# A graph kernel with lists of edges: two more anchors in each list, other windows of nodes per slot, and U copied bank by bank

## The chip, the cores and the metric

The kernel runs on one core of one Trainium2 chip. The metric is the device time of one execution, in microseconds (us). Before the change it is 1675.7 us, the median of three runs (1673.89, 1675.7 and 1681.47).

## What is computed

`reference` takes x (8 graphs' worth of features on 2048 nodes, 64 features each) and one adjacency matrix, 2048 x 2048, which is symmetric, has every node's own edge, and holds about nine ones in a row. Four layers follow each other, each as `x = layernorm(x + layer(x))`:

```
layer 0: h = layernorm((x*w + b + x) @ W);  att = softmax over the neighbours of leaky(s1[i] + s2[j]);  elu(att @ h + h)
layer 1: per feature: softmax over the neighbours of softplus(x)*wa;  sum of it times softplus(x)
layer 2: relu(x @ W_self + mean over the neighbours of x @ W_neigh), layer norm
layer 3: four heads h = x @ Wh[k].T;  softmax over the neighbours of h_i . h_j;  leaky;  @ Wo.T;
         then the same attention once more with one head; leaky; layer norm
```

The layer that matters here is the third, above all its four heads: for each edge (i, j), graph and head the score h_i . h_j, its exponential, and the weighted sum of x_j.

## The kernel before, in words

**Tiles, groups, slots.** The 2048 nodes are cut into 16 tiles of 128 (`NT`, index `it`), a tile into two groups of 64 nodes (`NG`, `g`), a group into two blocks of 32 (`GB`). The edges of a group are listed in 5 slots (`GS`, `s`) of 128 places each. A slot may hold only edges of the nodes in its window, `WINDOWS[s]`, given as first and last-plus-one node of the group (line 69): 20, 22, 24, 22 and 20 nodes. Windows overlap, since how many places a node needs depends on the data. `blocks_of(s)` tells which blocks a window touches: the first two slots the first block, the last two the second, the middle slot (`MID`) both.

**The listing** (lines 364 to 430) runs once over the 16 tiles. It loads 128 rows of the adjacency matrix, makes `on` and the degree `deg` of each node on ScalarE (line 368), finds each node's neighbours with VectorE's MAX8 (380 to 387), and works out `offs`, the place at which each node's list begins. TensorE sums the degrees of the nodes ahead with a matmul of the constant matrix `before` (396); VectorE clips that and adds `base` (397, 398). The first block of a group is so packed from the first place on, without holes, and the second one up to the last place. From `offs` come the selection matrices `SelT` and `Sel` (405 to 417) and `src`, the node numbers of all places (419 to 427). `node_products` (line 287) makes layer 0's rows every second tile. The order of instructions in this stage is made by a scheduler from dependences and priorities. All later stages gather the rows of neighbours from tables in DRAM by `src` (`gather`, line 203, on GpSimd's queue), so they start when the listing is through.

**The stages behind it** are layer 0, layer 1, layer 2, the heads of layer 3, and its last attention (`fifth`). In all of them but the heads the work on a slot is done for whole blocks of 32 nodes, whatever its window.

**The heads** (line 1039 on) are written in an order by hand (`manual_schedule`), engine by engine. Steps are (it, g, s), with the slots of a group in the order `TURN = (0, 2, 1, 4, 3)`. Two steps make a pair, and five pairs (j = 0 to 4) an iteration, that is one tile. In window sizes before: pair 0 has slots of 20 and 24 nodes, pair 1 22 and 20, pair 2 22 and 20, pair 3 24 and 22, pair 4 20 and 22. A pair does this:

- `score` (line 1092), twice: TensorE multiplies the gathered rows (`xsT`, the stationary operand, 64 rows by 128 columns) with `U` of the window's nodes, four heads by `ni` nodes as moving columns (line 1101); ScalarE takes the exponential into `w` (1104), VectorE clips and masks it (1107).
- `turn` (1085): 16 transposes of the rows of the next pair (line 713) and their copy by ScalarE (1088).
- a quarter of the work on whole nodes (`QUARTERS`): `wo_all` in pair 0 (1193), `through_w` in pairs 1 and 2, `sides` in pairs 3 and 4 (their matmuls are all line 1064, of `quarters`).
- `back` (1112), twice: TensorE multiplies `w` of each block of the window (moving columns: four heads by the nodes of the window in that block) with the gathered rows (line 1126).

`sides` makes U for the next tile, two heads at a time: `pu` has two PSUM banks (first index j), each with both heads. ScalarE copies the first head out of both banks (1073), then VectorE the second head (1074). `pscore` has two buffers (`ps_s`), which the two scores of a pair and the quarters use in turn. `w` has four buffers of one pool.

`look` (line 1543) counts nodes that don't fit: those whose list begins ahead of its windows or ends behind them, and groups with more than 640 edges. If there is one, a slow path (line 1635 on) computes everything again.

Of the kernel before, what the change touches and what calls it, by code (L numbers as in the profile page):

```python
# [21 lines left out]
F32 = mybir.dt.float32  # L22
# [5 lines left out]
AF = mybir.ActivationFunctionType  # L28
ALU = mybir.AluOpType
# [3 lines left out]
P = 128  # L33
# [15 lines left out]
def kernel(ctx: ExitStack, tc: tile.TileContext, ins: dict, out: bass.AP):  # L49
    nc = tc.nc  # L50
# [16 lines left out]
    SL = 24  # L67

    WINDOWS = [(0, 20), (10, 32), (20, 44), (32, 54), (44, 64)]

    def blocks_of(s):

# [9 lines left out]
    MID = GS // 2  # L82
# [8 lines left out]
    ident = const.tile([P, P], F32, name="ident")  # L91
# [3 lines left out]
    ones_col = const.tile([P, 1], F32, name="ones_col")  # L95
# [35 lines left out]
    main = fast.enter_context(tc.tile_pool(name="main", bufs=1))  # L131
# [55 lines left out]
    room = main.tile([P, 2], F32, name="room")  # L187


    SelT = main.tile([P, NT, GE], FP8, name="SelT")  # L190
# [40 lines left out]
    aw = adj_.enter_context(tc.tile_pool(name="adjw", bufs=1, reuse_waits="tile"))  # L231
    ap_ = adj_.enter_context(tc.tile_pool(name="adjp", bufs=2, reuse_waits="tile"))
# [54 lines left out]
    def node_products(t0, wk, ps):  # L287
# [26 lines left out]
        for q, ph in enumerate(held):  # L314
# [21 lines left out]
    before = aw.tile([P, P], F32, name="before")  # L336
# [3 lines left out]
    block_no = aw.tile([P, P // GB, GB], F32, name="block_no")  # L340
# [5 lines left out]
    part = aw.tile([P, 4], F32, name="part")  # L346
# [17 lines left out]
    for it in range(NT):  # L364
# [70 lines left out]
    wk = l0.enter_context(tc.tile_pool(name="l0k", bufs=2, reuse_waits="tile"))  # L435
# [114 lines left out]
    with ExitStack() as l1:  # L550
        wp = l1.enter_context(tc.tile_pool(name="l1w", bufs=1, reuse_waits="tile"))
        wk = l1.enter_context(tc.tile_pool(name="l1k", bufs=2, reuse_waits="tile"))
# [116 lines left out]
        n = 0  # L669
# [127 lines left out]
    with ExitStack() as l2:  # L797
        wp = l2.enter_context(tc.tile_pool(name="l2w", bufs=1, reuse_waits="tile"))
        wk = l2.enter_context(tc.tile_pool(name="l2k", bufs=2, reuse_waits="tile"))
# [193 lines left out]
        with tc.manual_schedule(engines=engines):  # L993
# [49 lines left out]
    with early, ExitStack() as heads:  # L1043
        wk = heads.enter_context(tc.tile_pool(name="f3s", bufs=2, reuse_waits="tile"))
# [8 lines left out]
        Us, os, xss, xsTs, ws, pos, h2s, zs, dTs, Rs, hTs = ({} for _ in range(11))  # L1053
# [14 lines left out]
        def sides(it, h0):  # L1068
            pu = quarters(G, lambda h: xTs[it].rearrange("p (a n) -> p a n", n=P), (h0, h0 + 1))
            if h0 == 0:  # L1070
                Us[it] = wk.tile([P, NP, HN, P], F32, name="U")
            U = Us[it].rearrange("p (j a) h n -> p j a h n", j=2)
            nc.scalar.copy(U[:, :, :, h0], pu[:, :, 0])
            nc.vector.tensor_copy(U[:, :, :, h0 + 1], pu[:, :, 1])  # L1074

        TURN = (0, 2, 1, 4, 3)
        steps = [(it, g, s) for it in range(NT) for g in range(NG) for s in TURN]
# [14 lines left out]
        def score(k):  # L1092
            it, g, s = steps[k]
            i0, ni = g * GN + WINDOWS[s][0], WINDOWS[s][1] - WINDOWS[s][0]
            pscore = ps_s.tile([P, 2, CW], F32, name="pscore")
            xsT = xsTs.pop(k)
            for p in range(NP):
                for k_ in range(2):
                    half = slice(k_ * D, (k_ + 1) * D)
                    f0 = p * HN * ni  # L1100
                    nc.tensor.matmul(pscore[:, k_, f0:f0 + HN * ni].rearrange("p (h i) -> p h i", i=ni),  # L1101
                                     xsT[half, p], Us[it][half, p, :, i0:i0 + ni], start=True, stop=True)
            w = ws[k] = wk.tile([P, 2, NP, HN, ni], F32, name="w", bufs=4)
            nc.scalar.activation(w.rearrange("p k a h i -> p k (a h i)"), pscore[:, :, 0:NP * HN * ni], AF.Exp)  # L1104
            edge = Sel[:, it, g].rearrange("p q n -> p (q n)")[:, FROM[s]:FROM[s] + ni].unsqueeze(1).to_broadcast([P, NP * 2 * HN, ni])
            wt = w.rearrange("p k a h i -> p (k a h) i")
            nc.vector.scalar_tensor_tensor(wt, wt, 3.0e38, edge, op0=ALU.min, op1=ALU.mult)  # L1107
# [197 lines left out]
        with tc.manual_schedule(engines=engines):  # L1305
# [11 lines left out]
            for m in range(len(steps) // 2):  # L1317
                it, j = divmod(m, PER)
# [42 lines left out]
    with ExitStack() as fifth:  # L1361
# [17 lines left out]
        hss, hsTs, pes, ws, wxs, zs, stats, sums = ({} for _ in range(8))  # L1379
# [163 lines left out]
        def look():  # L1543
            many_recs(8, last_recs)
            nc.vector.tensor_reduce(nbad[:, 9:10], few[:, 0:NT - 1], AX.X, ALU.add)
            nc.vector.tensor_scalar(nbad[:, 9:10], nbad[:, 9:10], float((NT - 1) * RD), None, op0=ALU.not_equal)
            lack = fp.tile([P, 5, NT], F32, name="lack")
            nc.vector.tensor_tensor(lack[:, 0], listed, deg, ALU.not_equal)
            nc.vector.tensor_tensor(ends, offs, deg, ALU.add)
            nc.vector.tensor_scalar(lack[:, 1], ends, room[:, 1:2], None, op0=ALU.is_gt)  # L1550
            nc.vector.tensor_scalar(lack[:, 3], offs, room[:, 0:1], None, op0=ALU.is_lt)
            crowd = fp.tile([P, NG, GN], F32, name="crowd")
            nc.vector.tensor_copy(crowd, group.unsqueeze(2).to_broadcast(crowd.shape))
            pc = ps_t.tile([P, NT], F32, name="pt")
# [80 lines left out]
    with tc.If(bad > 0), ExitStack() as anyway:  # L1635
        main = anyway.enter_context(tc.tile_pool(name="gmain", bufs=1))
# [25 lines left out]
        with tc.tile_pool(name="adjp", bufs=3) as ap_, tc.tile_pool(name="adjps", bufs=4, space=PSUM) as aps:  # L1662
# [19 lines left out]
            deg = small.tile([P, NT], F32, name="deg")  # L1682
# [489 lines left out]
```

## Time and profile before

| | |
|---|---|
| median of three runs | 1675.7 us |
| the profiled execution | 1810.59 us, its span 1808.8 us |
| mean granted TensorE clock in it | 0.861 |
| busy: TensorE, VectorE, ScalarE, GpSimd | 1378.3, 1195.8, 905.6, 782.8 us |
| listing | from 0 to about 182 us |
| layers 0, 1, 2 | to about 455, 704 and 953 us |
| heads | from about 953 to 1425 us |
| last attention | to the end |

The profiled execution took 135 us more than the median run. Busy times are of each engine's instructions, waits not counted; "PE" is TensorE's matmuls, "PEld" its loads of the stationary operand, DVE VectorE, ACT ScalarE, POOL GpSimd, and L1101 is line 1101 of the kernel. A group of instructions is given as line, engine, operation, what it writes and reads, shape, count, and then busy time and mean duration, and behind the second bar the idle time of the engine ahead of them with what ended it. One fp32 matmul of the program is two MATMUL records in the trace.

### The profile page before, as it was taken

Reading aid. Unit: us, or ns where it says so; the run is one execution under the profiler, and the core shown is the slowest. Engines: PE = TensorE matmul, PEld = TensorE weight load, DVE = VectorE, ACT = ScalarE, POOL = GpSimd, SP = SyncE. Lnnn points to the kernel's source line nnn. Section 1 sums busy time; section 2 is a strip of 40 time slices with the busy share of each in tenths; the row PEclk is TensorE's granted clock in tenths of the full one; section 3 lists DMA queues with packets and bytes.
Section 4 is the critical chain, followed back from the end, with each engine's and each line's share of the span. In section 5 each row is a group of like instructions: output and inputs, shape, how many; then the busy total and the mean of one; then the engine's idle time right before and its main releaser. Section 6 shows DMA issues by size and latency. Waiting matters only on the chain.

```text
span 1808.8 us, 39940 instructions
## 1 busy us (share of the span) xinstructions
PE 1378.3 (76%) x16028; PEld 949.9 (53%) x16028; DVE 1195.8 (66%) x2973; ACT 905.6 (50%) x1863; POOL 782.8 (43%) x777
## 2 busy tenths in 40 slices
PE   4673455653489996888937999999999779889993
PEld 3662233331133332732216777777777657667773
DVE  5989378787576465754763666666667626656667
ACT  5763133535961233535653556555655424555564
POOL 0000666662464552656624333334334056656551
PEclk9665667666799998999967999999999969998897
DMA  6550665552126883256614656665656266666651
GB/s 185 184 160 24 182 179 175 174 175 60 70 105 214 305 309 126 94 153 177 184 46 119 160 155 164 161 160 156 170 155 165 76 198 171 186 179 176 182 152 44
DMA packets 157019, 280.71 MB, mean 155 GB/s; under 512 B 68732, under 2 KB 94332, under 8 KB 154748
## 3 DMA queue, kind: packets, MB, share of 16 engines
q0 software_dynamic: 56320, 189.44, 35.5%
q1 hardware_dynamic: 83866, 84.45, 15.8%
q10 hardware_dynamic: 16640, 4.20, 1.0%
q8 instruction: 128, 2.10, 0.5%
q14 instruction: 65, 0.53, 0.1%
HBM read 237.60 MB, written 40.42 MB: 154 GB/s over the span
## 4 chain that ended last, share of the span: by engine, by line
PE 48%; ACT 8%; DVE 7%; issue 5%; DMA 1%; another core or an unknown queue 1%; POOL 1%; SPq 0%; ACTq 0%; POOLq 0%; DVEq 0%
PE pscore L1101 9%; PE pa L605 6%; PE po L1126 5%; PE ps L1429 5%; PE po L1468 4%; PE pt L1406 3%; PE pa L660 2%; PE pt L713 2%; ACT w L1104 2%; PE pa L1003 2%; PE pscore L1064 2%; PE py L833 2%; PE pe L1399 2%; PE pscore L1193 2%; ACT xsT L1088 1%
## 5 line engine op out<-in xcount | busy, mean ns | idle before, releaser
L204 POOL DMA_INDIRECT xs<-xtab,src x160 | 172.9, 1081 | 282.0 <-PE po L1126 243.9
L204 POOL DMA_INDIRECT hs<-htab,src x160 | 153.1, 957 | 261.7 <-PE pe L455 182.9
L204 POOL DMA_INDIRECT hs<-ktab,src x160 | 158.6, 992 | 139.4 <-DMA utab<-hT 46.3
L605 PE MATMUL pa<-R,ET 128*128 128x512 bf16 x768 | 179.4, 390 | 49.9 <-POOL R L593 33.7
L1107 DVE SCALAR_TENSOR_TENSOR w<-w,Sel 128x640 f32<-128x640 f32 (+2 forms) x160 | 134.2, 875 | 104.7 <-ACT w L1104 104.5
L1104 ACT ACTIVATE w<-pscore 128x640 f32<-128x640 f32 (+2 forms) x160 | 113.6, 745 | 145.5 <-PE pscore L1101 139.9
L1101 PE MATMUL pscore<-U,xsT 64*128 64x80 f32 (+2 forms) x2560 | 163.6, 278 | 5.4 <-DVE U L1074 4.3
L605 PEld LDWEIGHTS <-ET 128*128 128x128 fp8e4 x768 | 74.7, 100 | 162.5 <-issue 83.3
L170 ACT ACTIVATE X<-X,ln_m,ln_r 128x64 f32<-128x64 f32 x256 | 87.2, 427 | 144.3 <-DVE ln_m L162 134.0
L1101 PEld LDWEIGHTS pscore<-U,xsT 64*128 64x128 f32 x2560 | 152.6, 191 | 11.6 <-DVE U L1074 6.9
L1126 PE MATMUL po<-w,xs 128*64 128x88 f32 (+2 forms) x3072 | 130.8, 237 | 14.4 <-DVE w L1107 5.3
L1126 PEld LDWEIGHTS po<-w,xs 128*64 128x64 f32 x3072 | 113.8, 139 | 48.0 <-DVE w L1107 25.6
L1468 PE MATMUL po<-hs,w 128*32 128x65 f32 x2048 | 87.3, 234 | 33.2 <-issue 25.3
L1429 PE MATMUL ps<-U,hsT 128*128 128x64 f32 x768 | 104.3, 287 | 9.0 <-ACT hsT L1407 4.8
L1429 PEld LDWEIGHTS ps<-U,hsT 128*128 128x128 f32 x768 | 102.8, 210 | 10.0 <-ACT hsT L1407 5.4
L204 POOL DMA_INDIRECT rs<-rtab,src x80 | 75.8, 948 | 63.4 <-PE pa L660 43.0
L614 DVE RECIPROCAL rec<-pa 128x256 f32<-128x256 f32 x32 | 54.4, 1734 | 64.6 <-PE pa L660 30.8
L1468 PEld LDWEIGHTS po<-hs,w 128*32 128x32 f32 x2048 | 70.8, 118 | 45.0 <-issue 33.4
L1407 ACT COPY hsT<-pt 128x512 f32<-128x512 f32 x96 | 52.5, 586 | 81.8 <-remote 46.4
L476 DVE TENSOR_TENSOR hs<-hs,w 128x1024 f32<-128x1024 f32 x80 | 91.8, 1213 | 1.2 <-ACT wm L464 0.4
L204 POOL DMA_INDIRECT rs<-ytab,src x80 | 76.9, 961 | 32.9 <-issue 17.1
L1516 ACT ACTIVATE z<-z,ln_m,ln_r 128x64 f32<-128x64 f32 x240 | 83.4, 432 | 14.7 <-DVE ln_m L1504 14.1
(634 smaller groups left out, 3087.4 us busy)
## 6 DMA issues: line engine op xcount, KB each, us to landing
at<-in_adj SPq DMA_DIRECT2D x16, 1024.0 KB
R<-itab SPq DMA_DIRECT2D x60, 256.0 KB
rtab<-r SPq DMA_DIRECT2D x16, 512.0 KB
ptab<-hp SPq DMA_DIRECT2D x16, 384.0 KB
hi<-ptab SPq DMA_DIRECT2D x16, 384.0 KB
ktab<-hb SPq DMA_DIRECT2D x16, 260.0 KB
X<-in_x ACTq DMA_DIRECT2D x16, 256.0 KB
htab<-H SPq DMA_DIRECT2D x16, 256.0 KB
```

The source lines that it names most:

```text
L170: nc.scalar.activation(v[:, b], v[:, b], AF.Identity, scale=rstd[:, k:k + 1], bias=nmr[:, k:k + 1])
L204: nc.gpsimd.indirect_dma_start(out=dst, out_offset=None, in_=table[:, :], in_offset=bass.IndirectOffsetOnAxis(ap=src[:, it, s, g:g + 1], a ...
L476: nc.vector.tensor_tensor(wx, wx, along(w[:, own].rearrange("p g b -> p (g b)")), ALU.mult)
L605: nc.tensor.matmul(po[h].rearrange("p a f -> p (a f)"), ET[:, jt, it * P:(it + 1) * P], R[:, jt, q, h].rearrange("p a f -> p (a f)"), star ...
L614: nc.vector.reciprocal(rec, po[h][:, 0])
L1101: nc.tensor.matmul(pscore[:, k_, f0:f0 + HN * ni].rearrange("p (h i) -> p h i", i=ni), xsT[half, p], Us[it][half, p, :, i0:i0 + ni], start ...
L1104: nc.scalar.activation(w.rearrange("p k a h i -> p k (a h i)"), pscore[:, :, 0:NP * HN * ni], AF.Exp)
L1107: nc.vector.scalar_tensor_tensor(wt, wt, 3.0e38, edge, op0=ALU.min, op1=ALU.mult)
L1126: nc.tensor.matmul(po[half, p, :, a - blk * GB:b - blk * GB], xs[:, f0:f0 + D], w[:, k_, p, :, a - WINDOWS[s][0]:b - WINDOWS[s][0]], start ...
L1429: nc.tensor.matmul(pscore[:, g, 2 * p:2 * p + 2], hsT[:, g, p], U[:, p, :, node_block(g, k)], start=False, stop=(p == NP - 1))
L1468: nc.tensor.matmul(po[node_block(g, k), j, b], w[:, g, t], hs[:, g, t], start=(s == BEGIN[k] and b == 0), stop=(s == END[k] and b == B // ...
L1516: nc.scalar.activation(v, v, AF.Identity, scale=r, bias=n)
```

## The change

Two things are changed.

**Windows and anchors.** The windows become 16, 18, 32, 18 and 16 nodes. So that every list falls into them, the first node at depth 16 or more in a block (depth counted from the group's outer edge) may not begin ahead of place 128, and that at depth 28 not ahead of place 256; in the second block the same holds from the other end. For this the listing has two more constant matrices (`far`), whose matmul with `deg` gives minus the degrees outside of the anchor, and `base` enters as a matmul of its own (`base_diag`) instead of an add. Per tile there are three fp32 matmuls of one column more on TensorE, one [128,1] ACTIVATE on ScalarE (`gap`), and on VectorE two scalar_tensor_tensor in place of one tensor_tensor. Ahead of the loop stand 20 instructions on VectorE (nine of them of 128x128) in place of one and one iota on GpSimd. `look` compares the end of the first block with the begin of the second one, with two small instructions more. In the heads, `w` of the middle slot gets a buffer of its own, and there is one.

**U bank by bank.** In `sides`, ScalarE copies one bank (both heads, p = 0 and 1 of U), VectorE the other one (p = 2 and 3).

```diff
-    WINDOWS = [(0, 20), (10, 32), (20, 44), (32, 54), (44, 64)]
+    ANCHORS = (16, 28)
+    WINDOWS = [(0, 16), (10, 28), (16, 48), (36, 54), (48, 64)]
...
-    base = aw.tile([P, 1], F32, name="base")
-    nc.vector.tensor_scalar(base, part[:, 3:4], float(GB), float(GE), op0=ALU.is_ge, op1=ALU.mult)
+    inward = aw.tile([P, NG, GN], F32, name="inward")
+    nc.gpsimd.iota(inward, pattern=[[0, NG], [1, GN]], base=0, channel_multiplier=0, allow_small_or_imprecise_dtypes=True)
+    inward = inward.rearrange("p g n -> p (g n)")
+    other = aw.tile([P, P], F32, name="other")
+    nc.vector.tensor_scalar(other, inward, -1.0, float(GN - 1), op0=ALU.mult, op1=ALU.add)
+    nc.vector.tensor_tensor(inward, inward, other, ALU.min)
...
+    for k, n in enumerate(ANCHORS):
+        far = aw.tile([P, P], F32, name=f"far{k}")
+        nc.vector.tensor_scalar(far, inward, float(n), None, op0=ALU.is_ge)
+        nc.vector.scalar_tensor_tensor(far, block_no.rearrange("p a b -> p (a b)"), part[:, 1:2], far, op0=ALU.is_equal, op1=ALU.mult)
+        nc.vector.tensor_scalar(depth[:, 4 + k:5 + k], depth[:, 0:1], float(n), -1.0, op0=ALU.is_lt, op1=ALU.mult)
+        nc.vector.tensor_scalar(far, far, depth[:, 4 + k:5 + k], None, op0=ALU.mult)
+        nc.vector.tensor_scalar(depth[:, 2 + k:3 + k], depth[:, 0:1], float(n), float(P * (k + 1)), op0=ALU.is_ge, op1=ALU.mult)
+        outer.append(far)
...
-        nc.tensor.matmul(poff, before, deg[:, it:it + 1], start=True, stop=True)
+        nc.tensor.matmul(poff, before, deg[:, it:it + 1], start=True, stop=False)
+        nc.tensor.matmul(poff, base_diag, ones_col, start=False, stop=True)
+        pouter = plist[:, CW // 2 - 2:CW // 2]
+        for k in range(2):
+            nc.tensor.matmul(pouter[:, k:k + 1], outer[k], deg[:, it:it + 1], start=True, stop=True)
+        gap = ap_.tile([P, 2], F32, name="gap")
+        nc.scalar.activation(gap[:, 0:1], pouter[:, 0:1], AF.Relu, bias=depth[:, 2:3])
         nc.vector.tensor_scalar(offs[:, it:it + 1], poff, -1.5 * GE, 2.0 * GE, op0=ALU.max, op1=ALU.min)
-        nc.vector.tensor_tensor(offs[:, it:it + 1], offs[:, it:it + 1], base, ALU.add)
+        nc.vector.scalar_tensor_tensor(gap[:, 1:2], pouter[:, 1:2], depth[:, 3:4], gap[:, 0:1], op0=ALU.add, op1=ALU.max)
+        nc.vector.scalar_tensor_tensor(offs[:, it:it + 1], gap[:, 1:2], depth[:, 1:2], offs[:, it:it + 1], op0=ALU.mult, op1=ALU.add)
...
-            U = Us[it].rearrange("p (j a) h n -> p j a h n", j=2)
-            nc.scalar.copy(U[:, :, :, h0], pu[:, :, 0])
-            nc.vector.tensor_copy(U[:, :, :, h0 + 1], pu[:, :, 1])
+            U = Us[it].rearrange("p (j a) h n -> p j a h n", j=2)[:, :, :, h0:h0 + 2]
+            nc.scalar.copy(U[:, 0], pu[:, 0].rearrange("p h a n -> p a h n"))
+            nc.vector.tensor_copy(U[:, 1], pu[:, 1].rearrange("p h a n -> p a h n"))
...
-            w = ws[k] = wk.tile([P, 2, NP, HN, ni], F32, name="w", bufs=4)
+            w = ws[k] = wk.tile([P, 2, NP, HN, ni], F32, name="w_mid" if s == MID else "w", bufs=1 if s == MID else 4)
...
-            nc.tensor.matmul(pc, crowd.rearrange("p g n -> p (g n)"), deg, start=True, stop=True)
-            nc.vector.tensor_scalar(lack[:, 4], pc, float(GE), None, op0=ALU.is_gt)
+            nc.vector.tensor_scalar(ends, ends, meet[:, 0:1], None, op0=ALU.mult)
+            nc.vector.scalar_tensor_tensor(ends, offs, meet[:, 1:2], ends, op0=ALU.mult, op1=ALU.add)
+            nc.tensor.matmul(pc, crowd.rearrange("p g n -> p (g n)"), ends, start=True, stop=True)
+            nc.vector.tensor_scalar(lack[:, 4], pc, 0.0, None, op0=ALU.is_gt)
```

More of the change, by code (lines that the diff above doesn't have):

```diff
@@ L187 @@
     room = main.tile([P, 2], F32, name="room")
+    meet = main.tile([P, 2], F32, name="meet")
     SelT = main.tile([P, NT, GE], FP8, name="SelT")
@@ L351 @@
                                    op0=ALU.is_equal, op1=ALU.mult)
-    base = aw.tile([P, 1], F32, name="base")
-    nc.vector.tensor_scalar(base, part[:, 3:4], float(GB), float(GE), op0=ALU.is_ge, op1=ALU.mult)
+    inward = aw.tile([P, NG, GN], F32, name="inward")
[4 more added lines that the diff above has]
+    nc.vector.tensor_tensor(inward, inward, other, ALU.min)
+    depth = aw.tile([P, 6], F32, name="depth")
+    nc.vector.tensor_scalar(depth[:, 1:2], part[:, 3:4], -1.0, float(GN - 1), op0=ALU.mult, op1=ALU.add)
+    nc.vector.tensor_tensor(depth[:, 0:1], depth[:, 1:2], part[:, 3:4], ALU.min)
+    nc.vector.tensor_scalar(depth[:, 1:2], part[:, 3:4], float(GB), -2.0, op0=ALU.is_ge, op1=ALU.mult)
+    nc.vector.tensor_scalar(depth[:, 1:2], depth[:, 1:2], 1.0, None, op0=ALU.add)
+    outer = []
+    for k, n in enumerate(ANCHORS):
[7 more added lines that the diff above has]
+    for k in range(2):
+        nc.vector.tensor_scalar(meet[:, k:k + 1], part[:, 3:4], float(GB - 1 + k), 1.0 - 2.0 * k, op0=ALU.is_equal, op1=ALU.mult)
+    base_diag = aw.tile([P, P], F32, name="base_diag")
+    nc.vector.tensor_scalar(depth[:, 5:6], part[:, 3:4], float(GB), float(GE), op0=ALU.is_ge, op1=ALU.mult)
+    nc.vector.tensor_scalar(base_diag, ident, depth[:, 5:6], None, op0=ALU.mult)
     over_one = aw.tile([P, 1], F32, name="over_one")
@@ L395 @@
         poff = plist[:, 0:1]
-        nc.tensor.matmul(poff, before, deg[:, it:it + 1], start=True, stop=True)
+        nc.tensor.matmul(poff, before, deg[:, it:it + 1], start=True, stop=False)
+        nc.tensor.matmul(poff, base_diag, ones_col, start=False, stop=True)
+        pouter = plist[:, CW // 2 - 2:CW // 2]
+        for k in range(2):
+            nc.tensor.matmul(pouter[:, k:k + 1], outer[k], deg[:, it:it + 1], start=True, stop=True)
+        gap = ap_.tile([P, 2], F32, name="gap")
+        nc.scalar.activation(gap[:, 0:1], pouter[:, 0:1], AF.Relu, bias=depth[:, 2:3])
         nc.vector.tensor_scalar(offs[:, it:it + 1], poff, -1.5 * GE, 2.0 * GE, op0=ALU.max, op1=ALU.min)
-        nc.vector.tensor_tensor(offs[:, it:it + 1], offs[:, it:it + 1], base, ALU.add)
+        nc.vector.scalar_tensor_tensor(gap[:, 1:2], pouter[:, 1:2], depth[:, 3:4], gap[:, 0:1], op0=ALU.add, op1=ALU.max)
+        nc.vector.scalar_tensor_tensor(offs[:, it:it + 1], gap[:, 1:2], depth[:, 1:2], offs[:, it:it + 1], op0=ALU.mult, op1=ALU.add)
         nc.vector.scalar_tensor_tensor(ends[:, it:it + 1], offs[:, it:it + 1], -2.0, deg[:, it:it + 1], op0=ALU.mult, op1=ALU.subtract)
```

## The prediction

> **What bounds the kernel now.** First the busy times by stretch: listing (two of its stretches), heads, last attention. Behind each engine's name in the heading stand its busy us and its instructions; then the granted clock.
>
> ```profile
> core 0: us, PE busy (x) PEld busy (x) DVE busy (x) ACT busy (x) POOL busy (x), PEclk, DMA share, GB/s
> 50.00:100.00 50.00, 35.86 (x255) 32.94 (x254) 40.59 (x195) 36.30 (x66) 0.00 (x0) 0.62 0.45 150
> 100.00:150.00 50.00, 28.67 (x175) 26.57 (x176) 47.26 (x227) 27.93 (x49) 0.00 (x0) 0.58 0.45 142
> 953.00:1425.00 472.00, 433.39 (x8538) 365.83 (x8538) 308.98 (x437) 270.85 (x372) 170.86 (x158) 0.98 0.58 153
> 1425.00:1808.70 383.70, 307.98 (x3924) 248.30 (x3924) 233.66 (x610) 184.94 (x457) 193.36 (x181) 0.87 0.55 155
> ```
>
> The listing is VectorE's: 47.3 of 50 us in its second third. The heads are TensorE's: 433 of 472 us at nearly full clock, while VectorE has 309 and ScalarE 271. So I ask for the heads' matmuls by shape.
>
> ```profile
> L1101 PE MATMUL pscore<-U,xsT 64*128 64x88 f32 x1024 | 70.2, 276 | 0.0
> L1101 PE MATMUL pscore<-U,xsT 64*128 64x80 f32 x1008 | 69.3, 278 | 4.3 <-DVE U L1074 4.3
> L1126 PE MATMUL po<-w,xs 128*64 128x88 f32 x1024 | 53.1, 246 | 1.7 <-DVE w L1107 1.7
> L1126 PE MATMUL po<-w,xs 128*64 128x48 f32 x1024 | 36.8, 225 | 2.2 <-DVE w L1107 1.8 <-issue 0.2
> L1101 PE MATMUL pscore<-U,xsT 64*128 64x96 f32 x496 | 33.5, 275 | 0.0
> ```
>
> The two lines that the windows touch behave differently. Per record, L1101 costs 69 ns busy at 80 and at 88 columns (and 68 at 96); L1126 costs 52 ns at 88 and 36 at 48. The start times of single matmuls say it more exactly. They run in twos side by side; from one such two to the next it is 111.8 ns in L1101 at 80, 88 and 96 columns alike, and in L1126 75.9 ns at 88, 69.2 at 80 and 58.3 at 48.
>
> Last the waits inside an iteration (waits of the heads, TensorE and VectorE), and how two of them look in time (timeline of pair 3 and of the end of pair 4):
>
> ```profile
> PE pscore L1064 <- ACT w L1104: 13.3, 32, 0.6
> PE pscore L1101 <- DVE U L1074: 4.3, 15, 0.4
> PE po L1126 <- DVE o L1110: 2.8, 5, 0.7
> DVE U L1074 <- ACT U L1073: 17.4, 30, 0.9
> ```
> ```profile
> 1243.44 1.46 ACT L1104 ACTIVATE w<-pscore 128x768 f32<-128x768 f32 x2 [0.72 <-PE pscore L1101]
> 1244.28 1.76 DVE L1107 SCALAR_TENSOR_TENSOR w<-w,Sel 128x768 f32<-128x768 f32 x2 [1.68 <-ACT w L1104]
> 1244.30 1.09 PE L1064 MATMUL pscore<-xT,G 64*64 64x256 f32 x16
> 1245.32 1.76 PE L1126 MATMUL po<-w,xs 128*64 128x48 f32 x48
> ...
> 1251.65 0.62 ACT L1073 COPY U<-pscore 128x512 f32<-128x512 f32 x1
> 1252.30 0.69 DVE L1074 COPY U<-pscore 128x512 f32<-128x512 f32 x1 [0.42 <-ACT U L1073]
> ...
> 1253.04 2.03 PE L1101 MATMUL pscore<-U,xsT 64*128 64x80 f32 x32 [0.28 <-DVE U L1074]
> ```
>
> In pair 3 the middle slot stands first: exponential, mask and `back` follow each other without slack (the mask of its first step ends at 1245.2, `back` starts at 1245.3). At the end of pair 4 VectorE's U copy waits for ScalarE's, and the next iteration's first score for VectorE's, once in 15 of 16 iterations.
>
> **What the Trainium skill says.** "TensorE: Matmul & The Clock Gate", section "Back-to-back issue gap", prices a warm matmul at N/2.4 + 2.5 ns. With N counted twice for fp32 this is 69.2 at 80 and 75.8 at 88 columns: the trace agrees. The same page, section "LDWEIGHTS (loading the stationary operand)": time goes by the columns of the weights, P/1.2, whatever the rows, so 107 ns for 128 and 53 for 64. The trace has 111.8 and 58.3, 5 ns more, as floors that don't move with the moving columns. So `score` is bound by loading its 128-column weights, and `back` has a floor of 58.3. "PSUM — Partial Sum Buffer", section "PSUM bank collisions raise a hardware error", says that two engines may not read one bank at once, other banks they may. The trace before shows the two U copies one behind the other; it can't show the second half.
>
> **The change, part by part.** Durations are of the profiled execution.
>
> *`back` (L1126).* Eight twos per block. Per group: two slots go from 80 to 64 columns (16 nodes x 4 heads), at 69.2 to the floor 58.3: 8 x 10.9 = 87 ns each. Two go from 88 to 72, 75.9 to 62.5 by the price: 8 x 13.4 = 107 ns each. The middle goes from 2 x 48 to 2 x 64 (55.8 by the price, under the floor): nothing. Sum 0.388 us a group, x32 = **-12.4 us** of TensorE's stream.
>
> *`score` (L1101).* 80 to 64 and 88 to 72 columns lie under the weights' 111.8; 96 to 128 gives 2 x 128/2.4 + 2.5 = 109.2, also under it: **0**. Bounds: if time went by columns, 32 fewer per group x 8 x 0.83 ns x 32 = -6.8; if the 128 columns ran beside nothing, +1 us.
>
> *Exponential and mask.* Their rows (640: 702 and 821 ns; 704: 755 and 889; 768: 811 and 957) give 0.85 and 1.06 ns a column; so 512: 0.60 and 0.69, 576: 0.65 and 0.75, 1024: 1.02 and 1.23 us. They lie beside TensorE except where it waits. By pair, medians of 13 to 16 iterations, us from the pair's first score:
> - Pair 0 (16, 32): the long mask comes second and ends at about 4.68 (was 4.47); its `back` is due at 4.86. Only -0.09, from `back`.
> - Pair 1: TensorE doesn't wait; -0.19.
> - Pair 2: the quarter waits for the first exponential (-0.10). Its second `back` waits for VectorE's copy of `po` behind both masks (ends 5.58, `back` at 5.75); exponential and masks shorter move it -0.35. With its own -0.09: -0.44.
> - Pair 3 (32, 18): the long one is first. Exponential +0.21, mask +0.27, and `back` stands right behind: +0.48; -0.11 from the second `back`: **+0.37**.
> - Pair 4: quarter -0.10, `back` -0.19, and the U wait.
>
> *U.* By the order of the changed program VectorE's copy still waits for ScalarE's, so the copies stay in a row. But the next score's first four matmuls now need ScalarE's bank alone, the other four VectorE's. Pair 4 would last 5.67 without the wait and lasts 6.05: 0.38. Afterwards ScalarE's copy ends at 5.07, VectorE's at about 5.86; the score starts at 5.36 and comes to its fifth matmul at 5.36 + 0.06 + 4 x 0.112 = 5.87. The wait goes, -0.38; by the waits' table 0.29 to 0.46. If VectorE came 0.3 later, a third of it would remain. Pair 4: -0.67.
>
> Sum per iteration: -0.09 - 0.19 - 0.44 + 0.37 - 0.67 = -1.02, x16 = **-16.3 us**. Of it -12.4 is stream, +7.7 the long slot ahead, and -11.6 shorter waits. `w_mid`'s one buffer costs nothing: its last reader is five steps back. If it did wait, TensorE would.
>
> *Listing.* VectorE: nine 128x128 instructions at about 0.2 us and ten small ones at 0.07, then 16 x 0.07: 2.5 + 1.1 = 3.6 us on the engine that bounds the stage (the iota on GpSimd is 0.27 us, and ready at 5 us). TensorE: three one-column products per tile, each two records with two 128-column loads, 0.22 us at full and 0.45 at half clock, +0.7 to 1.3 us between degree and `offs`. A new wait: `gap` on ScalarE waits for TensorE, and in its queue the next tile's `on` (2.0 us) and the ET copies stand behind it; VectorE then waits for `gap` with the MAX8s behind it. While MAX8s can fill, this is hidden; in the last two tiles nothing is left to fill (VectorE waits 3.8 us for `offs` in three places already): 2 x 1.5 = 3. The scheduler also puts the stage in another order. I take **+6.6 us**, with ends at 0 (the new order happens to be better) and +16 (1 us a tile).
>
> *`look`.* Two small instructions, 0.15 us each: +0.3 at most. *Gathers:* as many rows of the same size. 0.
>
> *Do the lists fit?* By the kernel's formulas on the reference's adjacency, no node falls outside its windows, before or after.
>
> **Sum:** -16.3 + 6.6 + 0.3 = -9.4: 1810.6 becomes 1801 in the profiled execution. That one is 135 us above the median, and nothing shows where. TensorE's stream keeps exact multiples of its clock in the profile, so I carry the difference over unscaled: 1675.7 - 9.4 = **1666**.
>
> **Rivals.**
> *Listing outweighs (slower).* VectorE standing at `gap` behind a 2.0 us `on`. It decides from (16.3 + 8.4)/16 = 1.5 us a tile; at 2.0 it is +32 - 16 = 1692. For it: the clock there is 0.6, and VectorE has only 3 us of slack in 50. Against: ScalarE is busy 28 of 50, and 2 us is the worst case.
> *The waits don't shrink (same).* The delay of the middle slot comes also in pair 0 and the waits in pairs 2 and 4 are set by semaphores, not by durations: -12.4 + 7.7 - 3 + 7 = 1675.
> *`score` shrinks too (faster):* -6.8 more, 1659. Against: three widths, one spacing.
> *The change doesn't do what it says:* a list overflows, and the slow path runs: thousands of us.
>
> **How the numbers follow.** Forecast 0.50 (1661 to 1672 by itself), `score` shrinks 0.12, waits don't shrink 0.24, listing outweighs 0.13, slow path 0.01. Half a per cent, 8.4 us, is about what a measurement can tell: 1667.3 to 1684.1 is "same". Faster: 0.34 + 0.12 = 0.46; same: 0.16 + 0.21 + 0.02 = 0.39; slower: 0.11 + 0.03 + 0.01 = 0.15. Both signs of the main doubt, and the listing's ends, give 1653 to 1681.
>
> **What would show it.** Right: L1126 at 64 columns with 58 ns and at 72 with 62; L1101 with 112 at every width; pair 3 longer, pairs 2 and 4 shorter; no wait of L1101's first score on U; heads about 16 us shorter, listing about 7 longer. Wrong: a spacing above 112 at 128 columns; pair 0 with a wait on the mask; a listing of over 200 us.

## The result: slower by 0.6%

The changed kernel takes **1688.46 us** (median of 12 runs, 1682.16 to 1693.28), the kernel before 1676.84 us (12 runs, 1673.89 to 1684.15): ratio 1.0060 [1.0042, 1.0077], or +10 us [+7, +13]. The prediction was 1666 us, in a range from 1653 to 1681.

One thing no number below can be read without: the kernel before takes 1674 to 1684 us on the chips of this comparison and of runs e8b to e17 ("the faster chips"), and 1811 to 1839 us on the one chip of runs e0 to e7 ("the slower chip") and in the profile that the prediction was worked out on. The table therefore sets the profile of the changed kernel beside a second profile of the kernel before, run e8b, which stands at the same level.

| us | before (e8b) | after | difference |
|---|---|---|---|
| start to the first gather of layer 0 (the listing) | 186.4 | 202.5 | +16.1 |
| from there to the heads' first score | 741.9 | 743.3 | +1.4 |
| heads, to the last product of `back` | 424.6 | 414.3 | -10.3 |
| to the end | 322.5 | 325.4 | +2.9 |
| span | 1675.3 | 1685.5 | +10.2 |

The second row and the last but one are not effects of the change: in eleven profiles on the faster chips, with either set of windows, these stretches are 742 to 746 and 321 to 325 us. Each column is one execution, and others differ by some us. In seven profiles of the changed listing the first gather starts at 197.5 to 202.8 us, in five of the old one at 184.5 to 189.2. The heads of the change take 413 to 420 us in five profiles on the faster chips, those of before 423 to 425 in four. An iteration of the heads (one tile) has a median of 26.53 us in e8b and 25.90 after, which is 10 us in sixteen.

The busy times by stretch, of the changed kernel (columns as before: behind each engine's name its busy us and instructions, then the granted clock):

```profile
core 0: us, PE busy (x) PEld busy (x) DVE busy (x) ACT busy (x) POOL busy (x), PEclk, DMA share, GB/s
50.00:100.00 50.00, 36.96 (x252) 33.37 (x252) 40.51 (x193) 35.03 (x65) 0.00 (x0) 0.57 0.48 154
100.00:150.00 50.00, 35.41 (x196) 33.44 (x193) 38.14 (x185) 26.49 (x49) 0.00 (x0) 0.57 0.41 131
...
945.50:1360.50 415.00, 405.06 (x8530) 347.37 (x8530) 301.74 (x436) 272.23 (x372) 166.60 (x157) 0.99 0.65 174
1360.50:1685.50 325.00, 280.51 (x3924) 233.71 (x3924) 234.79 (x613) 183.22 (x457) 192.92 (x181) 0.90 0.64 183
```

and the heads of the kernel before at the same level (e8b):

```profile
928.00:1353.00 425.00, 415.70 (x8530) 357.19 (x8530) 309.63 (x436) 276.34 (x372) 173.23 (x157) 0.99 0.64 170
```

In the heads TensorE is busy 416 of 425 us before and 405 of 415 after: its busy time fell by 10.6 us, the stage by 10. In the listing VectorE is busy for *less* of the stretch from 100 to 150 us than in either profile of before (38.1 of 50 us where it was 47.3), though it has more to do: it stands and waits.

The heads' matmuls by shape in the changed kernel:

```profile
L1133 PE MATMUL pscore<-U,xsT 64*128 64x64 f32 x1024 | 70.7, 277 | 1.3 <-ACT xsT L1120 1.1 <-issue 0.2
L1133 PE MATMUL pscore<-U,xsT 64*128 64x72 f32 x1024 | 68.6, 272 | 0.0
...
L1158 PE MATMUL po<-w,xs 128*64 128x72 f32 x1024 | 44.7, 229 | 0.5 <-DVE w L1139 0.5
L1158 PE MATMUL po<-w,xs 128*64 128x64 f32 x1024 | 43.5, 227 | 5.4 <-DVE o L1142 4.7 <-DVE w L1139 0.7
L1158 PE MATMUL po<-w_mid,xs 128*64 128x64 f32 x1024 | 36.9, 225 | 3.1 <-DVE w_mid L1139 2.8
L1133 PE MATMUL pscore<-U,xsT 64*128 64x128 f32 x512 | 36.6, 284 | 0.0
```

L1133 costs about 70 us per 1024 records at 64, 72 and 128 columns alike, as L1101 did at 80, 88 and 96: from one two to the next it is 112 ns everywhere. L1158 went from 53.1 to 44.7 us at the slots 1 and 3; its spacing is 62 to 63 ns at 72 columns and 58 at 64.

Where VectorE waits in the listing (first 200 us; us in total, times, longest), before (e8b):

```profile
DVE SelT L406 <- ACT apart L405: 5.4, 4, 2.4
DVE offs L397 <- PE pl L396: 3.6, 4, 3.0
```

and after:

```profile
DVE offs L428 <- ACT gap L427: 12.2, 10, 2.6
DVE SelT L438 <- ACT apart L437: 10.5, 7, 3.0
```

VectorE waited for the offsets in four places, 3.6 us (3.0 of it in one); now it waits in ten, 12.2 us, and 5.1 us more for `apart`, which comes out of the offsets. That is 13.7 us more in these two rows, a part of it given back in others: up to the first gather VectorE's busy time rose by 6.1 us (149.8 to 155.9) and its idle time by 10.

### The profile page after: what moved, and what is told of

The parts are those of the page before. It is cut to its first block, busy times and chain, and to the rows that moved or that the text cites. A ratio compares the mean times of both kernels' runs of the same rounds, so it can differ in the third digit from the quotient of the medians.

```text
span 1685.5 us, 40154 instructions
## 1 busy us (share of the span) xinstructions
PE 1322.5 (78%) x16124; PEld 928.4 (55%) x16124; DVE 1195.7 (71%) x3010; ACT 910.0 (54%) x1879; POOL 780.4 (46%) x778
## 4 chain that ended last, share of the span: by engine, by line
PE 45%; DVE 11%; ACT 5%; issue 3%; POOL 3%; DMA 1%; SPq 0%; POOLq 0%; ACTq 0%; DVEq 0%
PE pscore L1133 9%; PE pa L637 6%; PE po L1158 6%; PE pscore L1096 4%; PE pt L745 3%; PE pa L692 3%; PE ps L1461 3%; PE py L865 2%; PE po L1500 2%; PE pscore L1225 2%; PE pt L1438 2%; PE pa L1035 1%; ACT z L902 1%; POOL hs L206 1%; DVE pr L1447 1%
## 5 line engine op out<-in xcount | busy, mean ns | idle before, releaser
L1133 PE MATMUL pscore<-U,xsT 64*128 64x64 f32 (+2 forms) x2560 | 162.3, 276 | 1.3 <-ACT xsT L1120 1.1
L1133 PEld LDWEIGHTS pscore<-U,xsT 64*128 64x128 f32 x2560 | 151.5, 190 | 5.4 <-ACT xsT L1120 1.3
L1136 ACT ACTIVATE w<-pscore 128x512 f32<-128x512 f32 (+1 forms) x128 | 79.7, 624 | 86.4 <-PE pscore L1133 84.9
L1139 DVE SCALAR_TENSOR_TENSOR w<-w,Sel 128x512 f32<-128x512 f32 (+1 forms) x128 | 92.3, 722 | 35.2 <-ACT w L1136 32.1
L1461 PE MATMUL ps<-U,hsT 128*128 128x64 f32 x768 | 96.6, 273 | 1.5 <-ACT hsT L1439 1.5
L1461 PEld LDWEIGHTS ps<-U,hsT 128*128 128x128 f32 x768 | 95.3, 197 | 1.8 <-ACT hsT L1439 1.7
L1035 PE MATMUL pa<-Y,ET 128*128 128x512 bf16 x384 | 90.2, 384 | 0.0
L1158 PE MATMUL po<-w,xs 128*64 128x64 f32 (+1 forms) x2048 | 83.1, 228 | 5.9 <-DVE o L1142 4.7
L1158 PEld LDWEIGHTS po<-w,xs 128*64 128x64 f32 x2048 | 70.4, 138 | 31.4 <-issue 16.8
L1120 ACT COPY xsT<-pt 128x1024 f32<-128x1024 f32 x80 | 80.9, 1012 | 9.8 <-PE pt L745 9.7
L1500 PE MATMUL po<-hs,w 128*32 128x65 f32 x2048 | 73.7, 226 | 4.6 <-DVE w L1473 4.6
```

Of the source, the lines that this page charges most:

```text
L1120: nc.scalar.copy(unflipped(xsT), pt.rearrange("p k s a n -> p k (s a) n"))
L1158: nc.tensor.matmul(po[half, p, :, a - blk * GB:b - blk * GB], xs[:, f0:f0 + D], w[:, k_, p, :, a - WINDOWS[s][0]:b - WINDOWS[s][0]], start ...
L1461: nc.tensor.matmul(pscore[:, g, 2 * p:2 * p + 2], hsT[:, g, p], U[:, p, :, node_block(g, k)], start=False, stop=(p == NP - 1))
L1500: nc.tensor.matmul(po[node_block(g, k), j, b], w[:, g, t], hs[:, g, t], start=(s == BEGIN[k] and b == 0), stop=(s == END[k] and b == B // ...
```

## Two theories

**A, the listing outweighs.** The three added products and `gap` lie in a chain that every tile goes through, and take more than the heads give. **B, the heads fail.** The listing costs the 6.6 us that were predicted, and the narrower windows and the U copies give nothing. Every ratio is to the kernel before, run beside it on the same chip; beside e0 to e3 the kernel before took 1831 us, beside e4 to e7 1818.

## The experiments

**e0, the kernel before again.**

> The kernel before once more, for a profile that stands near its median. Both theories: about 1677 us. Theory A (the listing outweighs): the first gather of layer 0 at about 185 us as in the first profile, so 17 us ahead of the changed kernel's 202.5, and an iteration of the heads of about 26 us, so that the heads win some 6 us of the 17 back. Theory B (the heads give nothing): the first gather at about 195 us, and an iteration of the heads no longer than the changed kernel's 25.5 us.

1838.2 us and not 1677, first gather at 189.2 us, heads 476.8 us. So the first profile was no accident of one execution: on this chip all 21 runs of the kernel before took 1822 to 1839 us. The waits that the prediction priced are here again (waits of TensorE in the heads):

```profile
PE pscore L1064 <- ACT w L1104: 15.5, 41, 0.6
...
PE po L1126 <- DVE w L1107: 5.0, 6, 1.3
...
PE pscore L1101 <- DVE U L1074: 4.0, 14, 0.4
```

**e1 and e17, the listing alone**: the changed kernel with the windows and copies of before.

```diff
-    WINDOWS = [(0, 16), (10, 28), (16, 48), (36, 54), (48, 64)]
+    WINDOWS = [(0, 20), (10, 32), (20, 44), (32, 54), (44, 64)]
...
```

> The kernel before with the anchors in the listing and the new comparison in the last check, but with the windows and the U copies of before. Theory A: the first gather at about 202 us and +17 us, ratio 1.010. Theory B: +6.6 us, ratio 1.004, as predicted for the listing.

> The listing of the change with the windows and U copies of before, once more. On a chip where the kernel before takes 1677 us, from the traces: +16 us in the listing and nothing elsewhere, ratio 1.0095. On the slower kind 1.0087 as before.

e1: 1.0087 [1.0061, 1.0114], +16 us. e17: 1.0116 [1.0092, 1.0140], +19.5 us [+15, +23], first gather at 202.1 us, heads 423.7 us as before. On the slower chip and on the faster ones the listing alone costs two to three times what was predicted; on the faster ones that is more than the whole change loses (1.0060), on the slower one the intervals overlap. Theory A holds; B's listing is refuted. Between e17 and the whole change lie some 9 us that the rest of the change wins, so the heads don't give nothing either.

**e2 and e15, the U copies alone**, in the kernel before.

```diff
-            U = Us[it].rearrange("p (j a) h n -> p j a h n", j=2)
-            nc.scalar.copy(U[:, :, :, h0], pu[:, :, 0])
-            nc.vector.tensor_copy(U[:, :, :, h0 + 1], pu[:, :, 1])
+            U = Us[it].rearrange("p (j a) h n -> p j a h n", j=2)[:, :, :, h0:h0 + 2]
+            nc.scalar.copy(U[:, 0], pu[:, 0].rearrange("p h a n -> p a h n"))
+            nc.vector.tensor_copy(U[:, 1], pu[:, 1].rearrange("p h a n -> p a h n"))
```

> The kernel before with only the U copies changed to one bank for each engine. The prediction's mechanism (the next score's fifth matmul waits instead of its first): -0.38 us in 15 of 16 iterations, -6 us, ratio 0.9965. If VectorE's copy still comes too late: 0, ratio 1.000.

> The kernel before with the U copies bank by bank, once more. On a chip where the kernel before takes 1677 us its trace has no wait of the first score for U: ratio 1.000. If the copies give something apart from that wait (or the chip is of the slower kind and the wait is there): 0.997.

e2: 0.9993 [0.9977, 1.0010]. In its trace pair 4 is 0.36 us shorter (6.13 to 5.77), as predicted, and pair 0 behind it 0.14 longer (6.26 to 6.40): the first exponential of pair 0 starts 1.84 us behind the first score, where it was 1.49. The interval leaves out the predicted 0.9965. e15: 0.9983 [0.9974, 0.9992], -2.9 us; pair 4 goes from 5.00 to 4.78, pair 0 stays. The wait for U, which the expectation of e15 missed on the faster chips, was there, on the loads of the stationary operand (waits of PEld in the heads of e8b), and it is gone in e15 and in the changed kernel:

```profile
PEld pscore L1101 <- DVE U L1074: 4.8, 15, 0.3
```

So the mechanism is right on both levels, and its size on the faster chips is 0.22 us an iteration and not 0.38.

**e3, the change without the U copies, and e4, the changed kernel again.**

> The changed kernel with the U copies of before. Theory A: 6 us longer than the changed kernel, 1694 us, ratio 1.010, if the U copies win what was predicted. Theory B: 1688 us or less, ratio 1.006, with the bank-by-bank copies worth nothing.

> The changed kernel itself beside the kernel before on this chip, for a profile that can be laid beside those of the parts. If the parts of the change add up (listing 1.0087, windows 0.999, U copies 0.9993): ratio 1.007. If the first comparison is the right one everywhere: 1.006. An iteration of the heads no more than 0.4 us shorter than the kernel before has it.

e3: 1.0078 [1.0053, 1.0104]. e4: 1.0071 [1.0046, 1.0096], the first comparison again. The intervals are too wide to tell the copies' part from these two.

**e5, `gap` on VectorE**, which takes ScalarE's queue out of the chain.

```diff
-        nc.scalar.activation(gap[:, 0:1], pouter[:, 0:1], AF.Relu, bias=depth[:, 2:3])
+        nc.vector.tensor_scalar(gap[:, 0:1], pouter[:, 0:1], depth[:, 2:3], 0.0, op0=ALU.add, op1=ALU.max)
```

> The changed kernel with the first step of the gap on VectorE (an add and a maximum in one instruction) in place of ScalarE. Theory A (VectorE waits behind ScalarE's queue in every tile): some 8 to 13 us of the listing's 16 come back, ratio to the kernel before 0.999 to 1.002, first gather at about 190 us. Theory B (the added instructions of VectorE and the other order of the stage are what costs): no gain or 1 us lost, ratio 1.006 to 1.008.

1.0112 [1.0078, 1.0147], first gather at 206.0 us (197.5 in e4). Nothing comes back: VectorE now waits for the products themselves (waits of VectorE in the listing):

```profile
DVE SelT L438 <- ACT apart L437: 15.1, 7, 5.3
DVE gap L427 <- PE pl L425: 11.8, 9, 1.8
```

This speaks against theory A in its first form, the queue behind ScalarE's `on`. e5 alone doesn't settle it, since the scheduler gave VectorE another order of instructions in it; e12 below does, with `gap` left on ScalarE. The second form of theory A is: the products are late.

**e6, another order of slots, and e7, without a long slot.**

```diff
-        TURN = (0, 2, 1, 4, 3)
-        OPEN, CLOSE = (0, 2), (1, 3)
+        TURN = (0, 4, 2, 1, 3)
+        OPEN, CLOSE = (0, 4), (1, 3)
```

> The changed kernel with the slots of a group in the order 0, 4, 2, 1, 3, so that the middle slot is first in pair 1 and second in pair 3 (it was second in pair 0 and first in pair 3). If the long slot ahead costs what pair 3 shows (0.5 us an iteration) and pair 1 has the slack that it shows, where TensorE waits for no mask: -8 us against the changed kernel, ratio to before 1.002. If the loss follows the slot into pair 1: no change, 1.007.

```diff
-    WINDOWS = [(0, 16), (10, 28), (16, 48), (36, 54), (48, 64)]
+    WINDOWS = [(0, 20), (10, 28), (20, 44), (36, 54), (44, 64)]
```

> The changed kernel with windows of 20, 18, 24, 18 and 20 nodes: the long slot is gone, slots 0 and 4 are as before, slots 1 and 3 keep their 18. Of the products' stream 6.8 us are saved and not 12.4. If the long slot ate the gain: -6.8 us in the heads against the listing alone, ratio 1.0087 - 0.004 = 1.005 or less. If something else holds the heads (the exponential's release): ratio 1.008 to 1.009.

e6: 1.0089 [1.0059, 1.0119]. Pair 1, which now has the long slot ahead, goes from 4.69 to 6.36 us, pairs 2 and 4 get 1.0 and 0.8 us shorter, and an iteration is 28.89 us, in e4 29.00 (medians): what pair 1 loses, pairs 2 and 4 win. e7: 1.0055 [1.0038, 1.0073], 28.97 us an iteration. Neither can be told from e4 by its time. But e7 gets there with a stream of products that is 5.6 us longer: without the long slot pair 3 takes 5.20 us and not 5.87, and the other pairs, with wider outer slots, give 0.70 us back. So on the slower chip the long slot costs about what the narrower outer slots win.

**e8b, e9b, e10b, e11b: the products in a place of their own.** `poff` and `pouter` lie in the tile of the lists (`pl`, one buffer), so the products of a tile can't start before the tile ahead has read its lists (`hit`). Here they lie in node_products' tile `pa_`; e10b does that to the kernel before, e11b has the windows of e7 besides. In all of them but e8b the scheduler also gave VectorE another order, so that place and order change together.

```diff
-        poff = plist[:, 0:1]
+        pfew = aps.tile([P, NP, 2, 2], F32, name="pa_", bufs=1)
+        poff = pfew[:, 0, 0, 0:1]
...
-        pouter = plist[:, CW // 2 - 2:CW // 2]
+        pouter = pfew[:, 1, 0, 0:2]
```

> The kernel before, for a profile from the same chip as the next three. No theory differs here: heads between 469 and 477 us from the first score to the last product, first gather at 185 to 189 us.

> The changed kernel with the degree products of the listing (offsets and the two anchors) in the PSUM tile of node_products (pa_) and not in the tile of the lists (pl). Theory A, second form (the products of a tile can't start before the previous tile's hit has read pl, and the chain from degree to SelT behind it is 2.4 us longer than before, in nine or ten tiles with nothing beside it): the products start behind the degree, gap is ready before MAX8 ends, VectorE no longer waits for it, 8 to 14 us come back, ratio to before 0.998 to 1.002, first gather at 184 to 190 us. Theory B (VectorE's own added work and TensorE's load at half clock): at most 2 us come back, ratio 1.006.

> The kernel before with the offsets' product in the tile pa_. Theory A, second form: the loop through pl gets 0.6 us a tile shorter here too, but VectorE is busy 47 of 50 us and waits for offsets only 3.8 us: -2 to -5 us, ratio 0.997 to 0.999. Theory B: 1.000.

> The previous but one with windows of 20, 18, 24, 18 and 20 nodes. If e7 was right that the long slot costs more than the narrower outer slots give: 3 us less than with the windows of the change, ratio 0.996 to 0.999; if not, the same or 3 us more.

e8b: 1677.06 us, heads 424.6, not the 469 to 477 that I had expected. e9b: 1.0030 [1.0021, 1.0040]: 5 us come back, less than expected. e10b: 1.0002 [0.9992, 1.0012], nothing, less than expected. e11b: 1.0035 [1.0024, 1.0046], the same as e9b. By the medians of an iteration, 25.97 us in e11b and 25.89 in e9b, the change's windows are the better ones by little over 1 us, and the stream would have said 5.6: here too the long slot costs most of what the narrower slots win (pairs 0 and 3 are 0.11 and 0.09 us shorter without it). In e9b VectorE no longer waits for the offsets, but for node_products, which now shares the tile:

```profile
DVE h_t L312 <- ACT pq L306: 8.1, 7, 2.9
...
DVE SelT L439 <- ACT apart L438: 6.9, 6, 1.6
```

**e12, e13, e14, e16: the products in bf16.** The matrices hold whole numbers that bf16 has exactly, and the degrees of this graph are at most 23; GpSimd, which has nothing to do between 50 and 150 us, converts the degree. In e12 the products stay in `pl`, so that nothing of the chain changes but the type and GpSimd's copy of the degree; in e13 they are in `pa_`, in e14 in the transposes' tile `pt`. e16 does the same to the one product of the kernel before.

```diff
...
-        nc.tensor.matmul(poff, before, deg[:, it:it + 1], start=True, stop=False)
-        nc.tensor.matmul(poff, base_diag, ones_col, start=False, stop=True)
+        deg_bf = ap_.tile([P, 1], BF16, name="deg_bf")
+        nc.gpsimd.tensor_copy(deg_bf, deg[:, it:it + 1])
+        nc.tensor.matmul(poff, before_bf, deg_bf, start=True, stop=False)
+        nc.tensor.matmul(poff, base_bf, ones_bf, start=False, stop=True)
...
-            nc.tensor.matmul(pouter[:, k:k + 1], outer[k], deg[:, it:it + 1], start=True, stop=True)
+            nc.tensor.matmul(pouter[:, k:k + 1], outer[k], deg_bf, start=True, stop=True)
```

> The changed kernel with the four constant matrices and the degrees of the listing in bf16 (all values are small whole numbers that bf16 holds), the degree copied to bf16 on GpSimd; the products stay in the lists' tile. If TensorE's fp32 products in the chain from degree to offsets are the rest of the cost: the chain is 1 us a tile shorter, VectorE's wait for gap falls from 12 to some 3 us, -8 us against the change, ratio to before 1.001. If only the place of the products counts: -1 us, 1.0055.

> As the run before, with the products in pa_ as in the run with their own bank (1.003 on the first kind of chip). If TensorE's time is the rest: ratio 0.998 to 1.000. If it is node_products' wait for pa_: 1.003 again.

> As the run before, with the products in the transposes' tile pt (two buffers), so that node_products' pa_ is free and VectorE's offsets stand among the MAX8s. If the wait for pa_ was the rest: 3 us better than with pa_, ratio 0.996 to 0.998, below the kernel before. If VectorE holding a pt buffer makes the transposes wait: no better than with pa_.

> The kernel before with its one product of the listing, degrees by the matrix before, in bf16. If the gain of the bf16 run came from the anchors' three products: VectorE waits 3.6 us for offsets here, so at most -3 us, ratio 0.998 to 1.000. If the listing is bound by its products altogether: -5 us or more, 0.997 or less.

e12: **0.9969 [0.9958, 0.9980]**, 1671.86 us: 15 us better than the change by the ratios, about twice what was expected, and 5 better than the kernel before. First gather at 185.5 us: the listing costs nothing more. Up to there the 779 instructions of VectorE and the 205 of ScalarE stand in the same order as in the changed kernel, so another order is not the cause. e13: 0.9975 [0.9964, 0.9985], no better than e12; beside e9b, which has the products in fp32 in the same place and the same order of VectorE, the first gather moves from 198.0 to 188.0 us. e14: 1.0053 [1.0033, 1.0072], worse: VectorE there waits 12.3 us for `sq`, which comes out of node_products' transposes; its order differs as well, so what makes it worse isn't shown. e16: 1.0010 [0.9995, 1.0025]: the kernel before gains nothing by it. So the gain of e12 is that of the products the change added, and e12 is the best kernel of the study.

The chain of the last tile in time shows it. In the changed kernel (timeline of the listing's end: start, duration, instruction; in brackets the wait ahead):

```profile
190.11 0.40 DVE L456 SCALAR_TENSOR_TENSOR hit<-hit,pl 128x240 f32<-128x240 f32 x1
...
190.65 0.56 PE L421 MATMUL pl<-deg,before 128*128 128x1 f32 x2 [2.03 <-DVE nbr L410]
...
191.07 0.56 PE L422 MATMUL pl<-ones_col,base_diag 128*128 128x1 f32 x2
191.43 0.97 PEld L425 LDWEIGHTS pl<-deg,far 128*128 128x128 f32 x4
191.49 0.99 PE L425 MATMUL pl<-deg,far 128*128 128x1 f32 x4
192.58 0.26 ACT L427 ACTIVATE gap<-pl,depth 128x1 f32<-128x1 f32 x1 [3.38 <-PE pl L425]
192.88 0.16 DVE L428 TENSOR_SCALAR offs<-pl 128x1 f32<-128x1 f32 x1 [1.66 <-ACT gap L427]
192.95 0.22 DVE L410 MAX8 nbr<-tops 128x8 f16<-128x64 f16 x1
```

and in e12:

```profile
174.67 0.40 DVE L465 SCALAR_TENSOR_TENSOR hit<-hit,pl 128x240 f32<-128x240 f32 x1
...
175.21 0.16 PE L430 MATMUL pl<-deg_bf,as_bf 128*128 128x1 bf16 x1 [2.03 <-DVE nbr L417]
...
175.26 0.19 PE L434 MATMUL pl<-deg_bf,as_bf 128*128 128x1 bf16 x2
...
175.55 0.26 ACT L436 ACTIVATE gap<-pl,depth 128x1 f32<-128x1 f32 x1 [1.78 <-PE pl L434]
...
175.85 0.16 DVE L437 TENSOR_SCALAR offs<-pl 128x1 f32<-128x1 f32 x1
```

In both, the products start 0.14 us after `hit` of the tile ahead is done. From the first product to the offsets it is 2.23 us in fp32 and 0.64 in bf16, with the same `gap` on ScalarE between; VectorE stood 1.66 us in the one, with a MAX8 behind the offsets in its order, and less than 0.1 in the other. In the whole stage its wait for the offsets falls from 12.2 to 1.5 us, the one for `apart` from 10.5 to 6.6:

```profile
DVE SelT L447 <- ACT apart L446: 6.6, 5, 2.1
...
DVE offs L437 <- ACT gap L436: 1.5, 2, 1.0
```

## Why the prediction was wrong, step by step

**"The listing is VectorE's".** Half right. VectorE is the busiest engine, but it is busy 149.8 of 186.4 us (e8b), and by the prediction's own table only 40.6 of 50 in the stretch from 50 to 100 us. Each tile also goes once through hit, products, offsets, `apart`, SelT, lists, hit, on three engines, and this loop had little slack: with three more products in it VectorE was idle 10 us longer. (It was not the bound before: in e16 its one product is shorter, and nothing is gained.)

**Listing, +6.6 (0 to +16): this is the step that failed.** It is +16.1 us in the traces, +19.5 [+15, +23] in the time of the listing alone. TensorE's price was right: 0.45 us a product at half clock, so 1.3 us more a tile, where tile 15 shows 1.86 us for four products and the kernel before 0.6 for its one. VectorE's was short: 3.6 us for its added instructions, where the busy time shows 6.1. The two new instructions of a tile take 0.21 us each in place of one of 0.15, some 4 us in all, priced at 1.1. What failed is the sentence "while MAX8s can fill, this is hidden; in the last two tiles nothing is left to fill". In VectorE's order the offsets come before the products are done in ten tiles of sixteen, and there it waits, with MAX8s behind it, 0.5 to 2.6 us and 1.2 on average, about what the products are longer. Two tiles times 1.5 us had to be ten times 1.2, and then `apart` as well. The place named, `gap` in ScalarE's queue behind `on`, was wrong too: e5 took ScalarE out and won nothing, e12 left it in, in the same order, and won all.

**`back`, -12.4.** The spacings came as priced (62 to 63 and 58 ns for 62.5 and 58.3). TensorE's busy time in the heads fell by 10.6 us.

**`score`, 0.** Right: 112 ns at 64, 72 and 128 columns. The Trainium skill, "TensorE: Matmul & The Clock Gate", section "LDWEIGHTS (loading the stationary operand)", says that loading goes by the weights' columns; the trace agrees, with 112 ns for 128-column weights whatever the moving columns from 64 to 128, and 58 ns for the 64-column weights of `back`.

**Waits and the long slot, together -3.9.** On the faster chips not there. They were priced pair by pair from a profile in which TensorE waits in the heads for exponentials, masks and U. On the faster chips its matmuls hardly wait. Their waits in the heads of e8b, whole:

```profile
PE po L1126 <- DVE w L1107: 3.0, 7, 0.8
PE pscore L1101 <- ACT xsT L1088: 1.1, 1, 1.1
PE po L1126 <- issue: 0.9, 1, 0.9
PE po L1126 <- DVE o L1110: 0.6, 1, 0.6
```

By pairs (e8b and after, medians; predicted change, measured change, us): pair 0 -0.09, **+0.11**; pair 1 -0.19, **-0.20**; pair 2 -0.44, **-0.09**; pair 3 +0.37, **-0.03**; pair 4 -0.67, **-0.42**. Pair 1, where only the stream counted, is right. In pair 0 the long mask ends at 4.93 and not at 4.68 (VectorE begins the first mask at 3.11 us of the pair, in e8b at 2.78, and in e15, with the new U copies alone, at 2.99), and `back` of the middle slot waits 0.1 us for it. In pair 2 the shorter first `back` only means a longer wait for VectorE's copy of `po`, which ends at 4.29 us as before; that is the wait of 4.7 us at L1158. In pair 3 the quarter's matmuls run until 3.48 us and cover the long exponential and all but 0.02 us of its mask. In pair 4 the U wait was 0.22 us.

On the slower chip, at the level of the profile that the prediction was read from, e3 (the change without the U copies) differs from e0, by one profile of each, by -0.04, -0.28, -0.37, +0.57 and -0.11 us in pairs 0 to 4, where -0.09, -0.19, -0.44, +0.37 and -0.29 were predicted. All signs are right there, but the long slot ahead in pair 3 costs more and pair 4 gives less: -3.7 us in sixteen iterations instead of -10.2. So the long slot was priced too low at that level.

The heads sum to -10.3 us for -16.3: about -3.3 of it the U copies (-2.9 [-1.3, -4.4] in e15, -6.1 predicted) and -7.0 the windows (-10.2 predicted, -12.4 by the stream alone). Two of the signs named for being wrong have come: a wait on the mask in pair 0 and a listing of over 200 us.

**"I carry the difference over unscaled."** This holds for the streams, whose spacing is the same in the first profile and in e8b (112 and 76 ns), and not for waits. That 135 us stood between the profile and the median was a sign that the waits in it were not those of the median.

**The rivals.** "Listing outweighs" gave the right sign, from 1.0 us a tile instead of the 1.5 that it was said to need, since the heads gave less, and for another reason than the one given. "The waits don't shrink", with some -8 us for the heads, came nearer to their -10.3 than the forecast's -16.3. It took both.

**Sum.** Predicted -16.3 + 6.6 + 0.3 = -9.4. Measured by the parts: listing +19.5, U -3, and the windows what is left of +10, -6.5; by the traces +16.1 - 10.3 + 4.4 = +10.2. Of the miss of some 20 us in the traces, 9.5 are the listing's, 6 the heads' and 4 lie in the stretches that the change leaves alone.

## What to carry to other kernels

A link added to a loop that every tile goes through counts once a tile, until the trace shows for each tile what hides it; that another engine is busier is no such proof. Before you shift work around a wait, look at what is late ahead of the engine that the profile names: here it named ScalarE, and the cost was TensorE's. And waits may be priced only from an execution that stands where the median stands.

## What was not expected of the hardware

In tile 15 four one-column products with fp32 weights of 128x128 took 1.86 us (changed kernel), the four in bf16 0.27 us (e12), both at a granted clock of 0.50. In this chain of small steps the type was worth 15 us in the same place and order; another place for the fp32 products brought 5 us, together with another order.

On the slower chip and on the faster ones the heads' matmuls run at the same spacing and at a granted clock of 0.98 to 0.99, and yet an iteration with the windows of before is 29.3 to 30.0 us on the one and 26.5 on the others (heads over sixteen). On the slower chip the first exponential of pairs 2 and 4 starts 2.67 and 2.60 us behind the pair's first score (e0), on the faster ones 1.18 and 1.17 (e8b), while the last product of that score is recorded as ended at 1.13 and 1.12 us in both (this end is modelled by the profile). In pair 2 of tile 7 (`it` = 7) the signal that the exponential waits for is recorded 1.8 us behind that end in e0 and 0.02 us behind it in e8b. So the time goes between the product and the signal, not in the exponential. Why, no run here tells; it stays open.
